# Weight loads ahead of the x loads on two queues, matmuls on zeros before them, and the matmuls for u moved behind the first transposes

## The chip, the cores and the metric

The kernel runs on one core of one Trainium2 chip. The metric is the device time of one execution in microseconds (us); lower is better. Six runs of the kernel before gave a median of 2239.54 us, from 2237.07 to 2243.34.

Names used throughout: PE is TensorE (matmuls and transposes; PEld is its weight load), DVE is VectorE, ACT is ScalarE, POOL is GpSimd, SP is SyncE. SP and ACT each issue DMAs through a hardware queue of their own, POOL through a software queue. Each engine works through its instructions in the order in which they stand in the program.

## The reference

Two layers over 3327 nodes with 512 features. `adj` is a dense 3327 x 3327 matrix.

```python
# layer 0: attention, with adj added twice to the scores
h = maximum(layernorm(x), 0)
q, k, v = h @ Wq.T + bq, h @ Wk.T + bk, h @ Wv.T + bv
a = q @ k.T / sqrt(512) + adj + adj
x = x + softmax(a) @ v
# layer 1: graph convolution
h = maximum(layernorm(x), 0)
A2 = adj + eye
temp = A2 @ h @ W.T
x = x + relu((d[:, None] * A2 * d[None, :]) @ temp)   # d = diagonal(A2) ** -0.5
```

The kernel folds q and k together: the scores need h (Wq.T Wk) h.T, so it forms the 512 x 512 product M = Wq.T Wk once (scaled), and a vector u = Wk.T bq (scaled) that carries the bias. bk adds the same number to a whole row of scores, so softmax drops it.

## The kernel before, in words

All of it is float32. Rows are padded to 26 tiles of 128. The large products (projection of h by M, scores, the three products with adj) are done blockwise in seven products of sums and differences of half matrices in place of eight. That is why one operand always has a step beside the matmuls in which DVE forms sums or differences.

The stages, in order:

1. **Start.** ACT's queue issues the loads of the first six tiles of x (`first`, line 276, 256 KB each). SP's queue issues `bq` (line 154), then the four 128-row pieces of Wq and of Wk in turn (line 285, 256 KB each), then a seventh tile of x, two blocks of adj (line 403, 384 KB each), and then the other 19 tiles of x.
2. **M and u.** PE forms M in 16 matmuls of 512 columns (line 292), with the weight piece `c` as the outer loop and four PSUM banks side by side, so that bank r is complete only in the last of four rounds. The trace shows two passes for each of these matmuls. ACT copies the banks to M in eight pieces (line 296). PE then does 16 one-column matmuls for u (line 300), DVE scales u (line 302), DVE forms four differences of blocks of M (`four_differences`, lines 177 to 180) and ACT negates M[0] in place (line 305). That negation must wait until line 177 has read M[0].
3. **h transposed, and projection.** `h_transposed(k)` (line 307) runs over the tiles of a pack (four packs, 26 tiles). Per tile: mean and variance on DVE (lines 191 to 195), the power on POOL (line 197), the bias `nb` on DVE (line 201), the normalized tile `ht` on ACT (line 314), its store from POOL (line 315), four PE transposes into one of two PSUM banks (line 318), and the copies and sums into `hp` on ACT and DVE (lines 321 to 327). `project_q(k)` (line 329) multiplies a pack by M in chains of products X, Y, Z (line 338), with results gathered on ACT and DVE (lines 343 and 346).
4. **Scores, attention and convolution.** These fill the rest of the time; the change touches none of their code.

Two rings set when the loads of x start: `x_ring` has seven slots, so the load of tile number n + 7 waits until ACT has read tile n at line 314; `n_ring` has four slots for `ht`, so the fifth `ht` waits until the first has been transposed and stored. (Tiles are counted here in the order of their use, from 0.)

The order on each engine is that of a scheduler in this part of the kernel; from the scores on it is fixed by hand. Two places of that order are used in the prediction's steps; they are the same in both kernels. On DVE, the statistics of tile 10 (line 191) with their small follow-ups (lines 193 and 195) stand ahead of the first difference of M (line 177); on ACT, the negation (line 305) stands ahead of the last two copies of M (line 296), and those ahead of the first copy of a transposed tile (line 321).

```python
    x_ring = ring(*((mid, k) for k in range(10, 15)), (half, 13), (half, 14))
    n_ring = ring(*((mid, k) for k in range(4)))
...
    for _ in four_differences(M):
        pass
    nc.scalar.mul(M[0], M[0], -1.0)
```

## Time and profile before

| What | Value |
|---|---|
| Median of 6 runs | 2239.54 us (2237.07 to 2243.34) |
| The profiled execution's own time | 2239.91 us |
| Its span, first to last instruction | 2237.7 us |
| Mean granted TensorE clock | 0.993 |
| DVE busy | 1623.6 us (73% of the span) |
| ACT busy | 230.8 us (10%) |
| DMA, read and written | 583.68 MB, mean 261 GB/s |

The profiled execution's span leaves 2.2 us of its time outside. Times in the trace count from the first instruction. A line of the timeline gives start, length, engine, source line, operation, output and inputs, size and count, and in brackets the idle time of the engine before it with what ended it. A group of instructions in a row is merged into one line; matmuls overlap, so a merged line's length is a little more than the distance to the next start. The view of waits gives, for a pair of waiting and releasing instruction, total time, number of times and the longest.

### The profile page before, as it was taken

The numbers are of one execution on the slowest core, as the hardware profiler recorded it, in microseconds if no ns is written. First come the engines' busy times: TensorE is split into PE (matmuls) and PEld (weight loads), VectorE is DVE, ScalarE is ACT, GpSimd is POOL, SyncE is SP. The second block draws the span as 40 slices with busy tenths as digits, with TensorE's granted clock in tenths as the row PEclk, the third lists the DMA queues.
The fourth block names the chain that finished last, engine by engine and source line by source line (L and its number), as shares of the span: only waits on it lengthen the run. The fifth ranks groups of instructions, "written<-read, shape, count | busy, mean of one in ns | idle before, by whom it ended". The sixth has DMA issues, their size and how long they took to land. (4 is left out here: it accounts for less than half of the span.)

```text
span 2237.7 us, 20973 instructions
## 1 busy us (share of the span) xinstructions
PE 2182.1 (98%) x6252; PEld 1162.8 (52%) x6252; DVE 1623.6 (73%) x3095; ACT 230.8 (10%) x336; POOL 357.0 (16%) x555
## 2 busy tenths in 40 slices
PE   8999999999999999999999999999999999999996
PEld 4555555455555555555444555555554555555553
DVE  6369888788878788877777778886543458776675
ACT  4321121112110000000000000000000000000011
POOL 4223333333321000001222110000000000000001
PEclk9999999999999999999999999999999999999998
DMA  6568888888969898888787899776646458765694
GB/s 246 205 216 301 297 293 285 303 284 303 349 210 331 325 371 287 286 290 279 244 302 240 301 342 354 276 277 205 207 123 205 146 165 304 231 209 175 210 307 147
DMA packets 246412, 583.68 MB, mean 261 GB/s; under 512 B 34770, under 2 KB 105904, under 8 KB 246288
## 3 DMA queue, kind: packets, MB, share of 16 engines
q1 hardware_dynamic: 191968, 399.15, 53.4%
q0 software_dynamic: 45104, 167.88, 19.8%
q10 hardware_dynamic: 9216, 15.21, 2.2%
q8 instruction: 52, 0.85, 0.2%
q14 instruction: 72, 0.59, 0.1%
HBM read 414.28 MB, written 167.85 MB: 260 GB/s over the span
## 5 line engine op out<-in xcount | busy, mean ns | idle before, releaser
L762 PE MATMUL p<-part,b 128*128 128x448 f32 (+1 forms) x3528 | 1255.9, 514 | 7.4 <-DVE part L172 6.2
L762 PEld LDWEIGHTS p<-part,b 128*128 128x128 f32 x3528 | 668.0, 190 | 575.6 <-issue 299.3
L171 DVE TENSOR_TENSOR part<-part 128x896 f32<-128x896 f32 (+1 forms) x252 | 256.6, 1018 | 84.5 <-PE p L762 46.7
L439 PE MATMUL Y<-qt,hp 128*128 128x448 f32 (+1 forms) x832 | 309.1, 514 | 4.4 <-DVE g L443 3.3
L439 PEld LDWEIGHTS Y<-qt,hp 128*128 128x128 f32 x832 | 157.1, 190 | 140.5 <-issue 72.3
L439 PE MATMUL Z<-qt,hp 128*128 128x384 f32 (+1 forms) x416 | 162.6, 513 | 0.0
L173 DVE TENSOR_TENSOR part<-part,part 128x448 f32<-128x448 f32 (+1 forms) x219 | 129.5, 591 | 17.4 <-PE p L762 0.9
L172 DVE TENSOR_TENSOR part<-part,part 128x448 f32<-128x448 f32 (+1 forms) x219 | 129.4, 591 | 7.3
L838 PE MATMUL p<-w,ct 128*128 128x512 f32 x272 | 125.5, 601 | 5.8 <-DVE part L850 4.1
L754 PE MATMUL p<-part,b 128*128 128x448 f32 (+1 forms) x336 | 124.2, 513 | 0.0
L439 PEld LDWEIGHTS Z<-qt,hp 128*128 128x128 f32 x416 | 78.8, 190 | 67.4 <-issue 36.2
L443 DVE SCALAR_TENSOR_TENSOR g<-g,Y 128x384 f32<-128x384 f32 (+1 forms) x156 | 91.4, 586 | 27.3 <-PE Y L439 26.2
L832 POOL DMA_DIRECT2D sum<-job x52 | 28.4, 547 | 486.0 <-DVE job L829 267.8
L797 DVE TENSOR_TENSOR part<-p,part 128x384 f32<-128x384 f32 (+1 forms) x33 | 19.3, 585 | 106.7 <-ACT part L796 57.4
L754 PEld LDWEIGHTS p<-part,b 128*128 128x128 f32 x336 | 63.5, 190 | 53.7 <-issue 32.6
L838 PEld LDWEIGHTS p<-w,ct 128*128 128x128 f32 x272 | 51.9, 192 | 67.7 <-issue 52.0
L796 ACT COPY part<-p 128x384 f32<-128x384 f32 (+1 forms) x33 | 16.5, 499 | 667.4 <-PE p L762 667.4
L439 PE MATMUL X<-qt,hp 128*128 128x384 f32 (+1 forms) x208 | 81.1, 512 | 0.0
L446 ACT ACTIVATE g<-g 128x768 f32<-128x768 f32 (+1 forms) x48 | 43.0, 896 | 353.9 <-DVE g L443 305.7
L838 PE MATMUL p<-w,part 128*128 128x512 f32 x144 | 68.1, 610 | 5.3 <-DVE ct L806 5.3
L431 POOL DMA_DIRECT2D sum<-o x52 | 36.8, 709 | 221.0 <-DVE o L425 155.4
L89 POOL DMA_DIRECT2D out_dram<-r x34 | 18.4, 542 | 306.8 <-DVE r L887 277.5
(157 smaller groups left out, 1867.5 us busy)
## 6 DMA issues: line engine op xcount, KB each, us to landing
part<-sum SPq DMA_DIRECT2D x104, 448.0 KB, 5.1
part<-p SPq DMA_DIRECT2D x91, 448.0 KB, 6.1
part<-sum SPq DMA_DIRECT2D x104, 384.0 KB, 3.5
part<-p SPq DMA_DIRECT2D x91, 384.0 KB, 4.2
part<-in_adjT_dram SPq DMA_DIRECT2D x78, 448.0 KB, 4.7
b<-row SPq DMA_DIRECT2D x234, 128.0 KB, 4.8
part<-in_adjT_dram SPq DMA_DIRECT2D x78, 384.0 KB, 3.7
g<-in_adjT_dram SPq DMA_DIRECT2D x52, 448.0 KB, 4.5
```

The costliest lines, as they stand in the source:

```text
L171: nc.vector.tensor_add(o[:, 0:2], g[:, 0:4:3], g[:, 1:2].to_broadcast([P, 2, g.shape[-1]]))
L172: nc.vector.tensor_add(o[:, 2], o[:, 1], g[:, 0])
L173: nc.vector.tensor_add(o[:, 3], o[:, 2], g[:, 2])
L431: nc.gpsimd.dma_start(self.to(sumd)[:, 0:2], self.o)
L439: nc.tensor.matmul(ps[:, :wd], h_of(self.t, name, k), qt[B[name]][:, k], start=start and k == 0, stop=k == 1, skip_group_check=True)
L443: nc.vector.scalar_tensor_tensor(a[n], a[n], 2.0, ps[:, :wd], op0=ALU.mult, op1=ALU.add if sign > 0 else ALU.subtract)
L446: nc.scalar.activation(g[1], g[1], AF.Exp, **({"bias": pad} if self.t == HALF - 1 else {}))
L754: nc.tensor.matmul(ps[("p2", "p3", "p4", "p8")[k]][:, :w], b[:, z], a[:, 0, y], start=k == 3, stop=True)
L762: nc.tensor.matmul(ps[r][:, :w], b[:, i], m, start=self.t == 0, stop=self.t == PAIRS - 1 and r in ("p1", "p5", "p6", "p7"))
L797: nc.vector.tensor_sub(c22, p["p6"], c11)
L832: nc.gpsimd.dma_start(sumd[self.s][self.j][:, 2 + self.k], self.a)
L838: nc.tensor.matmul(ps, cts[s][y][d][:, k * P : (k + 1) * P], w[d], start=d == 0, stop=d == DC - 1)
```

## The change

It has four parts. (a) The load of `bq` moves from the front of SP's queue behind the weights and x. (b) Wq is loaded from SP's queue and Wk from ACT's, first of all, and the first six tiles of x are put in pairs, one on each queue, behind the second, third and fourth pair of weight pieces. (c) DVE clears a 128 x 128 tile, and PE does eight matmuls of 128 columns on it into PSUM bank 5, which nothing reads. (d) The 16 matmuls for u and their scaling move behind the code of the first pack's `h_transposed`.

```diff
-    nc.sync.dma_start(bq_sb, bq)
...
-    first = {i: load_x(i, nc.scalar) for _, i in order[:6]}
...
+    first = {}
     for c in range(DC):
-        for w, src in ((w_q, wq), (w_k, wk)):
-            nc.sync.dma_start(w[c // 2][:, c % 2], src[c * P : (c + 1) * P])
+        for w, src, queue in ((w_q, wq, nc.sync), (w_k, wk, nc.scalar)):
+            queue.dma_start(w[c // 2][:, c % 2], src[c * P : (c + 1) * P])
+        if c > 0:
+            for (_, i), queue in zip(order[2 * c - 2 : 2 * c], (nc.sync, nc.scalar)):
+                first[i] = load_x(i, queue)
+    nc.sync.dma_start(bq_sb, bq)
...
+    zero = half(12, [P, P], "zero")
+    nc.vector.memset(zero, 0.0)
+    idle = bank(5, "idle")
+    for _ in range(8):
+        nc.tensor.matmul(idle[:, :P], zero, zero, start=True, stop=True)
     ps = [bank(k, "mm") for k in range(DC)]
...
-    pu = bank(4, "pu")
-    for r in range(DC):
-        for c in range(DC):
-            nc.tensor.matmul(pu[:, r : r + 1], w_k[c // 2][:, c % 2, r * P : (r + 1) * P], bq_sb[:, c : c + 1],
-                             start=c == 0, stop=c == DC - 1)
-    nc.vector.tensor_scalar(u, pu[:, :DC], scale, None, op0=ALU.mult)
...
     h_transposed(TURN[0])
+    pu = bank(4, "pu")
+    for r in range(DC):
+        for c in range(DC):
+            nc.tensor.matmul(pu[:, r : r + 1], w_k[c // 2][:, c % 2, r * P : (r + 1) * P], bq_sb[:, c : c + 1],
+                             start=c == 0, stop=c == DC - 1)
+    nc.vector.tensor_scalar(u, pu[:, :DC], scale, None, op0=ALU.mult)
```

In the order of the built programs, part (d) puts the matmuls for u behind the transposes of tiles 0 and 1, and the scaling of u behind the sums of tile 1 (lines 324 and 325). From the projection on, every engine has the same instructions in the same order in both kernels.

## The prediction

> **What bounds the kernel now.** I read the page first, then busy time by stretches, then PE's waits at the start, then the timeline of the first 40 us.

> ```profile
> span 2237.7 us, 20973 instructions
> ...
> PE 2182.1 (98%) x6252; PEld 1162.8 (52%) x6252; DVE 1623.6 (73%) x3095; ACT 230.8 (10%) x336; POOL 357.0 (16%) x555
> ```

> PE is busy for 98% of the span, so only PE's idle or slow time can be won. Busy time by stretches (length, then PE, PEld, DVE and so on) says how much of it lies where the change acts:

> ```profile
> 0.00:66.62 66.62, 54.31 (x221) 32.78 (x221) 41.89 (x147) 35.88 (x65) 30.63 (x60) 1.00 0.71 254
> 66.62:2237.70 2171.08, 2127.78 (x6033) 1130.06 (x6031) 1581.74 (x2950) 194.96 (x271) 326.36 (x496) 0.99 0.76 261
> ```

> Up to 66.62 us PE idles 12.31 us. After that it runs instructions that the change leaves in place, so whatever is won must be won here and then shifts all the rest. PE's waits in the first 75 us name those 12 us:

> ```profile
> PE mm L292 <- DMA wk<-in_wk_dram: 6.9, 1, 6.9
> PE tp L318 <- DVE hp L325: 2.3, 2, 1.9
> PE Z L338 <- DVE hp L324: 1.6, 1, 1.6
> PE tp L318 <- ACT hp L321: 1.0, 2, 0.8
> ```

> The first is what the change aims at. The timeline shows what follows it:

> ```profile
> 6.94 16.06 PE L292 MATMUL mm<-wk,wq 128*128 128x512 f32 x32 [6.94 <-DMA wk<-in_wk_dram]
> ...
> 10.48 0.34 PEld L292 LDWEIGHTS mm<-wk,wq 128*128 128x128 f32 x1 [0.52 <-issue]
> ...
> 11.25 0.19 PEld L292 LDWEIGHTS mm<-wk,wq 128*128 128x128 f32 x1 [0.43 <-issue]
> ...
> 20.55 0.69 DVE L191 BATCH_NORM_STATS2 st<-xt 128x6 f32<-128x512 f32 x1
> ...
> 22.01 0.69 DVE L177 TENSOR_TENSOR M<-M 128x512 f32<-128x512 f32 x1 [0.36 <-ACT M L296]
> ...
> 22.73 0.63 ACT L305 ACTIVATE M<-M 128x512 f32<-128x512 f32 x1
> 22.83 3.63 PE L300 MATMUL pu<-bq_sb,wk 128*128 128x1 f32 x32
> ...
> 26.32 1.07 PE L318 MATMUL tp<-ident,ht 128*128 128x128 f32 x8
> ...
> 26.99 0.58 ACT L321 COPY hp<-tp 128x512 f32<-128x512 f32 x1 [3.08 <-PE tp L318]
> ...
> 27.63 0.66 PE L318 MATMUL tp<-ident,ht 128*128 128x128 f32 x4 [0.24 <-ACT hp L321]
> ```

> Three things: the passes at line 292 start 0.85 us apart at first and 0.43 apart from 11.25 on, so PE ran at half rate for the first 4.2 us or so of its work; 32 passes took 15.89 us instead of 32 x 0.43 = 13.76. Second, the copy at 26.99 waited for PE, that is for u. Third, DVE reads tile 10 at 20.55, as it lands, and goes on to line 177 only then. That third thing hides behind u now; I think it decides the result.

> **The change part by part.**

> *Weights first.* The first weights land 3.7 us (Wq) and 5.2 us (Wk) after their issue, the second one at 6.8. They share the transfer with six tiles of x; landings come about 0.67 to 0.7 us apart (14 of 256 KB by 12.9). As the first pair on two queues from 0.74 on, they land where the first two transfers landed before: the first x at 3.7, the second landing at 4.9. [...] Later pairs, every 1.4 us or 2.8 with x between, are ahead of the 3.44 us that eight passes take.

> *Zero matmuls.* DVE's other memsets end at 0.99; the new one adds an estimated 0.15, before any x has landed. Eight matmuls are 16 passes of 128 columns. At the slow rate that is 0.855/4 = 0.21 each, by twice the 0.11 of the transposes 0.22: 3.5 us from about 1.3, to 4.85. So M starts at 4.9, not 6.94. If they ran at full rate, the landing sets it, 3.8 to 4.9; if each were twice as dear, 8.4, a loss of 1.5. The transposes' row is nearest, so 4.9. The clock: 4.2 us after 1.3 is 5.5, so (5.5 - 4.9)/2 = 0.3 us of loss remain of the 2.1. [...] I take 0.3. M ends at 4.9 + 13.76 + 0.3 = 19.0 instead of 22.83: 3.85 us won there.

> *u behind the transposes.* No work is saved: 32 passes, 3.49 us, only change places. The eight transposes come at 19.0 to 19.9, u to 23.4; then tile 2, which stood at 27.63. If nothing else held it, the gain would be 4.2. `bq` is needed at 19.9 and its landing, some 8 us earlier, is hidden. On DVE, u's scaling now stands behind tile 1's sums; behind it are two `nb`, which wait for POOL later anyway: nothing.

> *x behind weights: the price.* Tile 2's transposes need the bank that the copy at line 321 frees. On ACT that stands behind the negation (305), that behind DVE's line 177, that behind the statistics of tile 10. So when does tile 10 land? Before, `nb` for the first four tiles came after the sixth x (10.94); in the new DVE order it follows the fifth, on SP the seventh transfer, so about the fourteenth of all: 12.87 before, say 12.3 without the slow first us. `ht` of tile 0 then starts at 13.1 (11.81 before), that of tile 3 ends at 16.0 (14.74), and tile 10's load, which waits for it, is issued at 16.0:

> ```profile
> L272 SPq DMA_DIRECT2D xt<-in_x_dram x1: 328/328/328, 14.8 to 14.8; - x1
> ...
> DMA to landing us min/median/max: 5.8/5.8/5.8
> ```

> ```profile
> 10.00:20.00 10.00, 10.00 (x23) 4.31 (x22) 4.92 (x24) 2.93 (x4) 5.08 (x9) 1.00 1.04 391
> 20.00:30.00 10.00, 8.96 (x59) 6.76 (x58) 4.87 (x15) 6.02 (x15) 1.12 (x2) 1.00 0.02 6
> ```

> Those 5.8 us are a full queue (DMA share 1.04, then 0.02), not a latency. The amount in front of tile 10 is the same, so its landing moves less than its issue: bound 19.5 (queue never empty, 0.3 us won at the front and more overlap) to 21.8 (16.0 + 5.8). A small gap opens while x waits for `ht`; I take 20.3. POOL's powers for tiles 4 to 7, which wait for the later stores, let DVE arrive at about the same time. Then 1.1 us to line 177 (20.55 to 21.64 without its wait), 0.7 to the negation, 0.55 to the last copies of M, 0.6 of them: 23.25 for the copy at 321 instead of 26.99. Tile 2's transposes go at 23.25 + 0.6 = 23.9 instead of 27.63: **3.75 us**, 0.45 less than PE alone would give. From there ACT, DVE, POOL and the next loads follow tile 2 as before: the 0.80 us wait, the 1.61 at Z and the 2.3 later come back unchanged, with about 1 us of doubt in Z, where two loads took 5.0 and 4.4 us.

> *Sum:* 2239.91 - 3.75 = 2236.2 for the profiled execution, which is 0.37 above the median; against the median 2235.8. A measurement of this kernel tells about 0.2% (4.5 us) from no change, so the forecast lies just inside: the bound is 2235.06.

> **The rivals.**

> A, the sum above: gain 2.7 to 4.8, 2234.7 to 2236.8, chance 0.52. About 0.18 of that is a gain over 4.5, by a shorter wait at Z.

> B, tile 10 doesn't gate. It lands by 19.7, or DVE's wait disappears in part; PE's 4.2 us hold, and with loads less crowded a good part of the 1.61 us at Z goes: 5.0 to 6.5, about 2234. For it: the DMA engines stand idle from 21 to 28 us, so loads could be quicker. Against: they are full before. Chance 0.24.

> [...] With other half losses, chance 0.14.

> D, slower. Tile 10 lands so late that the copy at 321 comes after 26.99; each us from a landing of 24.0 on costs one us. That needs 8.0 us from its issue at 16.0, where the longest of the 256 KB loads took 6.0; or the fifth x at 14.5 and 6.0 on top of that. Landing at 27: 3 us lost, 2242.5. For it: three more loads in front of the fifth x. Chance 0.10, of which 0.06 over 0.2%.

> **How the numbers follow.** The likeliest is A: 2235.8. The range takes in B and C: 2233.0 to 2239.0, leaving D and the tail of B. Faster by over 0.2%: B and the good end of A, 0.42; slower 0.06; within 0.2%, 0.52.

> **What would show it.** First pass at line 292 near 4.9 us with PEld 0.19 long at once (step of the zeros); PE's first wait in the list gone; the next start after M's last pass near 19.0. Tile 10's statistics near 20.3 with DVE idle ahead of them, line 305 near 22, and a wait of about half a us of tile 2's transposes for the copy at 321. If that wait isn't there and tile 2 goes at 23.4, B. [...] If the copy comes after 27, D. I'd also be wrong if something after 66.62 us reacts to the shift.

## The result, and the profile after

The changed kernel takes 2235.68 us, the median of 32 runs (2229.05 to 2239.77). The kernel before, run beside it, takes 2239.83 us, the median of 69 runs. The ratio is 0.998, with a 95% interval of 0.9974 to 0.9986, which is a gain of 3.1 to 5.8 us. The forecast was 2235.8 us, 3.75 us less than before.

Line numbers move a little: in the changed kernel the matmuls for M are line 302 (292 before), M's copies 306 (296), the negation 309 (305), `ht` 318 (314), the transposes 322 (318), the copy out of their bank 325 (321), the sums behind it 328 and 329 (324 and 325), Z 342 (338). The zero matmuls are line 298, those for u line 368. DVE's first difference of M is line 176 and its statistics line 190.

The head of the page, after:

```profile
span 2232.6 us, 21006 instructions
...
PE 2184.5 (98%) x6268; PEld 1167.5 (52%) x6268; DVE 1622.6 (73%) x3096; ACT 230.9 (10%) x336; POOL 357.9 (16%) x555
```

PE is busy 2.4 us longer in a span that is 5.1 us shorter: the 16 zero passes are new work. Busy time by stretches, after (length, then PE, PEld, DVE, ACT, POOL, and at the end clock, DMA share and GB/s):

```profile
0.00:66.62 66.62, 60.78 (x244) 39.20 (x245) 43.80 (x150) 36.01 (x65) 31.42 (x61) 0.95 0.76 264
```

PE's idle time in the first 66.62 us falls from 12.31 to 5.84 us. These 6.47 us are not the gain: from 1.15 to 4.72 us PE now does zeros, 3.57 us that count as busy. And the mean clock is down from 1.00 to 0.95. The clock's first record stands at 11.14 us before and at 5.34 after, and this column counts what lies ahead of it as full: it doesn't show the slow start at all, and the drop to 0.95 is the first sign of something else, which the forecast lacked. PE's waits of the first 75 us, after:

```profile
PE tp L322 <- DVE hp L329: 2.1, 2, 1.7
PE Z L342 <- DVE hp L328: 1.4, 1, 1.4
PE idle L298 <- DVE mh L621: 1.1, 1, 1.1
PE tp L322 <- ACT hp L325: 1.1, 2, 0.7
```

The 6.9 us for `wk` are gone; in their place stands the 1.1 us until DVE's memsets are done, and everything below has hardly changed. PE's timeline, after:

```profile
1.15 3.78 PE L298 MATMUL idle<-zero 128*128 128x128 f32 x16 [1.15 <-DVE mh L621]
4.72 14.21 PE L302 MATMUL mm<-wk,wq 128*128 128x512 f32 x32
18.77 1.04 PE L322 MATMUL tp<-ident,ht 128*128 128x128 f32 x8
19.64 4.30 PE L368 MATMUL pu<-bq_sb,wk 128*128 128x1 f32 x32
24.34 1.11 PE L322 MATMUL tp<-ident,ht 128*128 128x128 f32 x4 [0.40 <-ACT hp L325]
```

M runs from 4.72 to 18.77 us. The passes for u take 4.30 us where they took 3.63. Tile 2's transposes, the last line, wait 0.40 us for ACT and start at 24.34 instead of 27.63 us: 3.29 us won there. What ACT and DVE do ahead of that is seen in their timelines, after:

```profile
20.91 0.69 DVE L190 BATCH_NORM_STATS2 st<-xt 128x6 f32<-128x512 f32 x1
...
21.93 0.68 DVE L176 TENSOR_TENSOR M<-M 128x512 f32<-128x512 f32 x1
```

```profile
22.64 0.63 ACT L309 ACTIVATE M<-M 128x512 f32<-128x512 f32 x1 [3.87 <-DVE M L176]
23.17 0.64 ACT L306 ACTIVATE M<-mm 128x256 f32<-128x256 f32 x2
23.70 0.59 ACT L325 COPY hp<-tp 128x512 f32<-128x512 f32 x1
24.17 0.40 ACT L327 COPY hp<-tp 128x256 f32<-128x256 f32 x1
24.43 0.84 ACT L318 ACTIVATE ht<-xt,nb,rstd 128x512 f32<-128x512 f32 x1
```

Tile 10 of x lands at 20.89, DVE takes it at once, and ACT stands still for 3.87 us until the first difference of M is done. Then ACT works without a gap. PE had filled the first bank by about 19.4 us; the copy out of it came at 23.70. So the chain from tile 10 to tile 2 is there as forecast. Busy time by short stretches, after, shows the lost clock:

```profile
20.00:22.00 2.00, 2.00 (x20) 2.00 (x20) 1.89 (x9) 0.00 (x0) 0.00 (x0) 1.00 0.40 151
22.00:23.00 1.00, 1.00 (x9) 1.00 (x8) 0.60 (x2) 0.36 (x1) 0.00 (x0) 0.71 0.00 0
23.00:29.00 6.00, 4.92 (x19) 3.91 (x20) 3.49 (x10) 5.29 (x12) 2.42 (x5) 0.50 0.39 103
29.00:30.00 1.00, 1.00 (x4) 0.44 (x4) 0.72 (x3) 1.00 (x2) 0.98 (x2) 0.88 0.87 336
```

The granted clock is at half from 22.41 to 29.24 us, 6.83 us long, beginning while PE works on u without a break. In the first profile of before it was full from 11.14 us on, up to 1065.86 us. The 3.29 us won at tile 2 shrink to 2.50 at the first Y (27.93 against 30.43). At the first Z they are 2.18 (34.73 against 36.91), but there PE waits for a load of x. DVE's timeline, after:

```profile
33.66 0.69 DVE L190 BATCH_NORM_STATS2 st<-xt 128x6 f32<-128x512 f32 x1 [1.58 <-DMA xt<-in_x_dram]
34.27 0.40 DVE L328 TENSOR_TENSOR hp<-hp,tp 128x256 f32<-128x256 f32 x1
```

These are the statistics of tile 13, which landed at 33.63, and the sums that Z needs stand behind them on DVE. In six profiles (this one, after_again, gate10, no_u_move, loads_only and zeros_only) the first Z starts 1.09 to 1.10 us behind the landing of tile 13. So 0.8 us, from tile 2 to Y, is what the half clock took here; what follows is set by a load. From 66 to 560 us the gain stays at 2.41 us.

The two profiled spans differ by 5.1 us, though, not 2.4. The rest comes later, in steps of up to 1.7 us in both directions. One cause is half-clock stretches of different length (near 2013 us, 6.83 us before and 3.41 after); not every step has one. Two executions of the changed kernel differ in the same way: the distance of after and after_again moves between -1.5 and +0.9 us behind 200 us. A single pair of profiles therefore shows where time went in the first 66 us; what the change is worth is read from the medians.

### The profile page after: what moved, and what is told of

Read it like the earlier page. It is cut to its first block, busy times and chain, and to the rows that moved or that the text cites. A ratio compares the mean times of both kernels' runs of the same rounds, so it can differ in the third digit from the quotient of the medians.

```text
span 2232.6 us, 21006 instructions
## 1 busy us (share of the span) xinstructions
PE 2184.5 (98%) x6268; PEld 1167.5 (52%) x6268; DVE 1622.6 (73%) x3096; ACT 230.9 (10%) x336; POOL 357.9 (16%) x555
```

## The experiments

The theory at the outset: (1) the early weights and the zeros win 3.85 us at M; (2) moving u wins nothing, because (3) tile 10's landing, through DVE's order and the negation, sets tile 2; (4) the half clock behind u takes about 1.2 us back. The rivals: the gain comes from the early loads or the zeros alone; moving u is needed; tile 10's gate costs little; the half clock has nothing to do with u.

A table of what all profiles show, in us from the first instruction. "Gate" is the landing of the tile of x whose statistics stand last ahead of the first difference of M (tile 10, but tile 9 in gate10, none in gate8 and its kin). "Copy" is the first copy out of the transposes' bank.

| Kernel | ratio to before (95% interval) | M starts | last of u | gate | negation | copy | tile 2 | half clock from, for |
|---|---|---|---|---|---|---|---|---|
| before | | 6.94 | 26.21 | 20.53 | 22.73 | 26.99 | 27.63 | none |
| before_again | | 7.41 | 26.46 | 21.24 | 22.99 | 27.25 | 27.89 | 28.24, 6.83 |
| after | 0.998 (0.9974 to 0.9986) | 4.72 | 23.59 | 20.89 | 22.64 | 23.70 | 24.34 | 22.41, 6.83 |
| after_again | one run | 4.72 | 23.57 | 21.31 | 23.06 | 24.12 | 24.76 | 21.96, 10.24 |
| loads_only | 0.9992 (0.9983 to 1.0001) | 4.56 | 25.18 | 21.31 | 23.36 | 26.53 | 27.17 | 23.17, 10.24 |
| zeros_only | 0.9988 (0.9979 to 0.9997) | 6.38 | 23.57 | 20.10 | 22.13 | 24.35 | 24.99 | 25.07, 6.83 |
| u_only | 0.9998 (0.9989 to 1.0007) | 6.61 | 26.09 | 20.45 | 22.20 | 23.27 | 26.20 | 26.54, 6.83 |
| no_u_move | 0.9981 (0.9972 to 0.9989) | 4.52 | 21.90 | 22.52 | 24.42 | 25.48 | 26.12 | 21.37, 10.24 |
| gate10 | 0.9973 (0.9965 to 0.9982) | 4.72 | 23.57 | 21.53 | 23.29 | 24.35 | 24.99 | 21.98, 10.24 |
| gate8 | 0.996 (0.9948 to 0.9972) | 4.72 | 23.59 | none | 19.98 | 21.05 | 23.80 | 22.35, 6.83 |
| gate8_again | 0.9957 (0.9944 to 0.997) | 4.72 | 23.60 | none | 20.08 | 21.15 | 23.81 | 22.54, 6.83 |
| gate8_wide32 | 0.9959 (0.9943 to 0.9975) | 4.43 | 25.16 | none | 20.86 | 21.93 | 22.57 | 24.59, 6.83 |
| no_move_wide | 0.9993 (0.9984 to 1.0002) | 4.72 | 22.19 | 21.15 | 23.19 | 24.25 | 24.89 | 29.15, 3.41 |

### The parts alone

**loads_only**: before with the new order of loads, parts (a) and (b). From the changed kernel:

```diff
-    zero = half(12, [P, P], "zero")
-    nc.vector.memset(zero, 0.0)
-    idle = bank(5, "idle")
-    for _ in range(8):
-        nc.tensor.matmul(idle[:, :P], zero, zero, start=True, stop=True)
...
+    pu = bank(4, "pu")
...
     for _ in four_differences(M):
...
     h_transposed(TURN[0])
-    pu = bank(4, "pu")
```

> Only parts (a) and (b): weights first on two queues, x between them, bq last; no zero matmuls, u in its old place. My theory: M starts when the first pair lands (4.3 us), at the half rate for its first 4 us or so (2.1 us lost), ends near 20.2; u to 23.7; the first copy of a transposed tile after that; tile 2's transposes near 25.0 instead of 27.63, so 2.7 us won there, total 2237.1. Rival (x behind weights delays all that follows): tile 2 at 27 or later, no gain. Rival (the loads bring everything): tile 2 near 24.3, as in the whole change, total 2236.

Measured: 2237.92 us, ratio 0.9992 (0.9983 to 1.0001). M started at 4.56 us and ended at 20.84, 0.3 and 0.6 us later than expected; full clock came only 4.96 us after its first pass. Tile 2 was forecast for 25.0 and came at 27.17: the half clock began at 23.17, so u took 4.56 us up to the first transpose (3.49 in the first profile of before), and the transposes came 0.22 us apart (0.11 in after, from 18.77 to 19.64). The early loads alone win 2 us at M. At the end the gain is between -0.2 and 3.8 us, which can't be told from nothing.

**zeros_only**: before with part (c).

```diff
+    zero = half(12, [P, P], "zero")
+    nc.vector.memset(zero, 0.0)
+    idle = bank(5, "idle")
+    for _ in range(8):
+        nc.tensor.matmul(idle[:, :P], zero, zero, start=True, stop=True)
     ps = [bank(k, "mm") for k in range(DC)]
```

> Only part (c): zero matmuls ahead of M, loads and u as before. My theory: M still waits for its weights until 6.9 us but runs at full rate from there, ends near 20.7 instead of 22.8; tile 2's transposes near 25.5: 2.2 us won there, total 2237.6. Rival (zeros do not wake the clock, or it falls asleep again in the 2 us before the weights land): M ends at 22.8, 0 won.

Measured: 2237.25 us, ratio 0.9988 (0.9979 to 0.9997), and tile 2 at 24.99 where 25.5 was expected. M started at 6.38 and its last pass at 19.76 us: 13.38 us for 31 distances, that is 0.43 each from the first on. The zeros do warm the clock, and that alone is a gain, of 0.7 to 4.7 us. (That M started 0.56 us earlier than in the first profile of before is an earlier landing in this execution; the loads are the same.)

**u_only**: before with part (d).

```diff
-    pu = bank(4, "pu")
...
     h_transposed(TURN[0])
+    pu = bank(4, "pu")
...
```

> Only part (d): u's matmuls behind the first transposes, loads as before, no zeros. My theory: PE's order costs nothing and wins nothing by itself but the wait of 0.24 us ahead of tile 2; tile 2's transposes near 27.2 instead of 27.63, total 2239.3, within the noise of before. Rival (the copies of the first tiles, done beside u now, take over the 0.8 us wait behind it too): 1.0 to 1.2 us won at the first product Y.

Measured: 2238.66 us, ratio 0.9998 (0.9989 to 1.0007). Copies at 23.27 wait for nothing that PE does any more, and tile 2 comes right behind u, at 26.20. A pass earlier or later there is nothing: u's 3.5 us only change places with the transposes. That the profile shows 1.4 us at tile 2, a us more than expected, comes with an M that ended 1 us earlier in this execution (last pass at 21.41 against 22.41): its weights landed 0.3 us earlier, and full clock came 2.86 us after its first pass instead of 4.20.

**no_u_move**: all but part (d). From the changed kernel:

```diff
+    pu = bank(4, "pu")
...
     for _ in four_differences(M):
...
     h_transposed(TURN[0])
-    pu = bank(4, "pu")
```

> The whole change without part (d): loads and zeros new, u in its old place ahead of the transposes. My theory (the first copy of a transposed tile is held by DVE's statistics of tile 10, not by PE): PE has u done by 22.3 and transposes tiles 0 and 1 by 23.2, in the shadow of that copy at 23.7; tile 2's transposes at 24.3, the same as in the whole change, total equal to it within 0.5 us (2235.7). Rival (moving u wins its share): tile 2 about 0.9 us later, at 25.2.

Measured: 2235.72 us, ratio 0.9981 (0.9972 to 0.9989), the same as the whole change. So moving u can't be told from nothing, both alone and on top of the rest; each time the interval is some 2 us wide to either side. Tile 2 came 1.8 us later in this profile than expected. PE was done with u and the first transposes by 24.1, well before the copy at 25.48; tile 10 had landed late, at 22.52, and DVE had waited for the tile before it:

```profile
21.89 0.69 DVE L190 BATCH_NORM_STATS2 st<-xt 128x6 f32<-128x512 f32 x1 [2.14 <-DMA xt<-in_x_dram]
...
23.70 0.68 DVE L176 TENSOR_TENSOR M<-M 128x512 f32<-128x512 f32 x1
```

The negation followed at 24.42, the copy at 25.48 (1.06 later) and tile 2 at 26.12 (0.64 later): the chain of the forecast with other numbers at its head.

Loads and zeros together are worth 0.0019, by these medians about what they are worth one by one (0.0008 + 0.0012, each with 0.0009 to either side).

### Is it tile 10 that gates?

**gate10**: the changed kernel with one ordering more on DVE: the statistics of tile 10 stand behind the sums of tile 1. Only these statistics and their small follow-ups change their place; up to 87 us nothing else does on any engine, as the traces show.

```diff
+    def newest():
+        return nc.cur_bb.bb.instructions[-1]
+
+    gates, seen = [], []
     def norm(src):
         nc.vector.bn_stats(st, src)
+        seen.append(src)
+        if len(seen) == LATE and gates:
+            tc.add_manual_dep(newest(), gates[0],
+                              mybir.DependencyInfo(mybir.DependencyClass.NoSync, mybir.DependencyReason.DATA),
+                              reason="behind the sums of tile 1")
...
                 nc.vector.tensor_add(hp[k][:, 5, :, w], hp[k][:, 0, :, w], pt[:, 0:2])
+                gates.append(newest().name)
```

Here `LATE` is 11, so tile 10 alone is moved.

> The whole change, with one difference in DVE's order: the statistics of tile 10 stand behind tile 1's sums and no longer ahead of the first difference of M; nothing is left out. My theory (DVE's wait for x holds the negation, that the copies of M, those the first copy of a transposed tile): the gate is tile 9 now, which lands about 1 us earlier. The negation follows tile 9's landing by 1.8 to 2.0 us as it followed tile 10's before; at a landing of 19.9 it is at 21.7, tile 2's transposes near 23.4 instead of 24.3. Total 0.5 to 1 below the whole change, about 2235. Rival (PE's own order holds tile 2): no change at tile 2.

Measured: 2234.34 us, ratio 0.9973 (0.9965 to 0.9982); its interval overlaps that of the change, so no gain is shown. Tile 2 was expected at 23.4 and came at 24.99, later than in the changed kernel: the loads of x were late in this execution, and tile 9 landed at 21.53, not at 19.9. But the gate passed on to tile 9 as expected: the negation came 1.76 us after its landing, where it had come 1.75 us after tile 10, and only 1.22 us after that of tile 10 (22.07), which no longer stands in its way. A different tile with the same distance speaks for the mechanism; gate8 tests it by taking the gate away.

**gate8**: the same with `LATE` at 9 and the condition `LATE <= len(seen) <= 11`, so that tiles 8, 9 and 10 stand behind the sums of tile 1. Tiles 0 to 7 have their statistics done before M is.

> As the last, with the statistics of tiles 8, 9 and 10 behind tile 1's sums; nothing is left out. My theory: nothing of DVE waits for x ahead of the differences; the negation comes at 18.5 to 19 (when ACT has M[0] and M[1] ready and tile 7's bias is done, by 19.5 at the latest), the first copy by 20.6, and now PE is what holds tile 2: its transposes follow u's last pass at 23.2 (23.7 if the clock falls to half in u). Total 1 to 1.5 below the whole change, about 2234.5. Rival (PE's order, or the statistics coming later cost as much): tile 2 at 24.3, or the first product Z later than in the whole change.

Measured: 2230.94 us, ratio 0.996 (0.9948 to 0.9972): 3.6 us below what was expected, better than both kernels, and its interval lies just apart from that of the change. ACT's timeline, gate8 (line 320 is the negation, 336 the copy, 329 `ht`):

```profile
19.98 0.63 ACT L320 ACTIVATE M<-M 128x512 f32<-128x512 f32 x1 [1.25 <-DVE M L177]
...
21.05 0.59 ACT L336 COPY hp<-tp 128x512 f32<-128x512 f32 x1
...
21.78 0.84 ACT L329 ACTIVATE ht<-xt,nb,rstd 128x512 f32<-128x512 f32 x1
```

The wait ahead of the negation falls from 3.87 to 1.25 us, though tile 10 landed at 20.89 us again: the negation, at 19.98, is now ahead of it. It still came 0.5 us later than the latest time expected. PE now sets tile 2: u's last pass starts at 23.59, tile 2's first at 23.80. That is only 0.54 us earlier than in the changed kernel, and yet the first Z starts at 32.99, 1.74 us earlier. The lead is 0.95 us at 55 us and 2.75 us from 66 us on. PE's waits of the first 75 us, gate8:

```profile
PE idle L309 <- DVE mh L633: 1.1, 1, 1.1
PE tp L333 <- DVE hp L340: 1.0, 1, 1.0
PE tp L333 <- ACT hp L336: 0.9, 2, 0.7
```

The 1.4 us at Z are gone. Gone too are the 1.7 us for line 329's sum, which PE waited at 61 us in the changed kernel; in return gate8 waits 1.0 us for such a sum at 52 us. One cause is in ACT's queue: `ht` of tile 4 stands behind the negation and the copies, at 24.43 us in the changed kernel and at 21.78 in gate8, and it frees the slot of `x_ring` for tile 11. That load is issued at 25.30 against 22.65 us, and the loads behind it are less crowded: tile 13, for which Z waited, lands at 31.49 instead of 33.63 us, though it is issued only 0.56 us earlier. The view of line 271 of the changed kernel, from 21 to 30 us, has who waited for these loads and the time from issue to landing:

```profile
  DVE st L190: 2.2, 2
...
DMA to landing us min/median/max: 2.7/4.4/5.0
```

In gate8 nobody waits for them, and the landing takes 3.1 us at the median. But there is a second cause, which this run can't separate from the first. The scheduler placed more than the three statistics differently, on all four engines behind 24 us: in gate8 tile 13's statistics stand at 36.11 us, behind the sums for Z (31.76), and no longer ahead of them. So a late negation costs 0.5 to 1 us at tile 2 (against after and after_again). That it costs again at Z by way of the ring is likely, and how much of the 1.4 us is not shown.

**gate8_again**: the same kernel once more.

> gate8 as before, beside the wider u on one chip and as a repetition: 2230.9 (ratio to the kernel before 0.996), negation not tied to the landings of tiles 9 and 10, tile 2's transposes 0.2 us behind u's last pass, near 23.8. If the first result owed something to its chip, the ratio comes out nearer to that of the whole change, 0.998.

Measured: 2231.47 us, ratio 0.9957 (0.9944 to 0.997), negation at 20.08, tile 2 at 23.81. It repeats, on another chip.

### Does u cost the clock?

**before_again**: the kernel before, once more, for its profile.

> The kernel before, unchanged, for a second profile. Theory of the clock: the half clock after u belongs to all versions and the first profile of before, which showed none, was the exception; here a stretch of 6.8 or 10.2 us at half clock begins between 23 and 30 us. Then the first product Y, at 30.4 in the first profile, is 1 to 2 us later. Rival (before never has it, the change brings it): full clock up to 1000 us, Y at 30.4 again.

Measured: 2241.62 us, one run. The stretch from 28 to 35 us, in this second profile of before:

```profile
28.00:35.00 7.00, 6.32 (x21) 4.39 (x22) 3.99 (x14) 5.02 (x10) 4.51 (x8) 0.52 0.65 213
```

The clock is 0.52 here, and 1.00 in the same stretch of the first profile. So the half clock behind u is no work of the change: four of the five profiles with u in its old place have it (this one, loads_only, zeros_only and no_u_move), and the first profile of before is the exception. It cost less here than expected: the first Y came at 31.18, 0.75 us later than in the first profile. Against this second profile the changed kernel is 2.4 + 2.7 = 5.1 us ahead at 100 us, against the first 2.4 us; the medians' 4.15 us lie between. Most of these 2.7 us are not the clock behind u: the two profiles of before differ by 0.7 us at 55 us, and the rest comes by 80 us, with longer waits of PE for DVE's sums (2.2 us in place of 1.9) and another half-clock stretch at 65.79 us.

**after_again**: the changed kernel, once more.

> The changed kernel once more, for a second profile of it. If the half clock behind u is a property of the kernel (one-column passes that leave TensorE nearly idle for the clock gate), a stretch of 6.8 or 10.2 us at half clock starts again between 21.4 and 25 us. If the first profile caught a chance event, there is none before 60 us. Tile 10 of x gates in both: negation = landing of tile 10 + 1.75 to 2.05 us, first copy = negation + 1.06, tile 2's transposes 0.6 later; by the landings seen so far (20.9 to 22.5) they start between 24.3 and 26.2. Its time: 2235.7, one run, so 2231 to 2240 says nothing.

Measured: 2233.99 us, one run. Half clock from 21.96 us for 10.24 us, negation 1.75 us behind tile 10, copy 1.06 later, tile 2 at 24.76: all as expected. Ten of the eleven profiles with u in one-column passes have the stretch.

**no_move_wide**: all but part (d), and u's matmuls 128 columns wide. The moving operand is the column of bq repeated 128 times, and one column of each result is used.

```diff
-            nc.tensor.matmul(pu[:, r : r + 1], w_k[c // 2][:, c % 2, r * P : (r + 1) * P], bq_sb[:, c : c + 1],
-                             start=c == 0, stop=c == DC - 1)
-    nc.vector.tensor_scalar(u, pu[:, :DC], scale, None, op0=ALU.mult)
+            nc.tensor.matmul(pu[:, r * P : (r + 1) * P], w_k[c // 2][:, c % 2, r * P : (r + 1) * P],
+                             bq_sb[:, c : c + 1].to_broadcast([P, P]), start=c == 0, stop=c == DC - 1)
+    nc.vector.tensor_scalar(u, pu[:, 0 : BW : P], scale, None, op0=ALU.mult)
```

> The whole change without part (d), and u's matmuls 128 columns wide (the same column read 128 times), of which one is used; nothing is left out. Theory of the clock: a stretch of PE with only one-column passes counts as idle, so that the clock falls to half after u (it did in five of six profiles: from 21.4 for 10.2 us in the kernel with one-column passes). With wide passes, which should take the same 0.11 us each, u counts as work: the clock stays full through u and 3.4 us more, so no half clock before 25.8, or none at all; total 1 to 2 below that kernel's 2235.7. Rival (the fall is a matter of chance or of other causes): half clock from 21 to 25 again, same total.

Measured: 2238.62 us, ratio 0.9993 (0.9984 to 1.0002). That is 4 to 5 us above what was expected, and above its kin no_u_move (0.9981), though the intervals overlap. The profiled execution, 2230.36 us, is the fastest of the 14. The passes started at 18.73 to 22.19 us, 0.11 us apart like the narrow ones. The stretch behind u, no_move_wide:

```profile
22.00:29.00 7.00, 3.14 (x26) 2.46 (x24) 4.67 (x17) 4.92 (x11) 2.31 (x4) 1.00 0.27 85
```

The clock stays full, though PE is busy for only 3.14 of these 7 us, where the changed kernel was busy for 4.92 of 6 us and had half. That speaks for the width of the passes as what counts, not for PE's busy time; a count in the last section bears it out. The 3.4 us that the expectation adds behind u are the author's estimate; 3.41 us is what the shortest half-clock stretch of after lasts, and here the half clock came 6.96 us behind the start of u's last pass. But it is one profile, a half-clock stretch comes later in it (29.15 us, behind these waits of PE), and its time can't be used: with the other operand the scheduler put the transposes, ACT's and DVE's steps around u in another order, and PE waited 1.56 us for the copy and 1.62 us for DVE's sums behind it. It doesn't show what the half clock behind u costs.

**gate8_wide32**: gate8, with u 32 columns wide; only PE's order changes, tile 2's transposes going between u's passes.

```diff
-            nc.tensor.matmul(pu[:, r : r + 1], w_k[c // 2][:, c % 2, r * P : (r + 1) * P], bq_sb[:, c : c + 1],
+            nc.tensor.matmul(pu[:, r * P : r * P + 32], w_k[c // 2][:, c % 2, r * P : (r + 1) * P],
+                             bq_sb[:, c : c + 1].to_broadcast([P, 32]), start=c == 0, stop=c == DC - 1)
-    nc.vector.tensor_scalar(u, pu[:, :DC], scale, None, op0=ALU.mult)
+    nc.vector.tensor_scalar(u, pu[:, 0 : BW : P], scale, None, op0=ALU.mult)
```

> gate8 with the matmuls for u 32 columns wide instead of one (the moving operand is bq's column repeated 32 times; only one column of each result is used). If it is the width of the moving operand that the clock gate counts, more work per pass shortens or removes the half clock behind u: full clock through 22 to 30 us, up to 1.5 us less than gate8, 2229.5. If 32 columns are still too few, the half clock stays as in gate8 (6.8 us from about 22.4) and the time is the same, 2230.9. A rival: the half clock has nothing to do with u; then also the same. u's passes stay at 0.11 us each in all cases; if they are longer, the time is up to 1 us more, 2232.

Measured: 2230.1 us, ratio 0.9959 (0.9943 to 0.9975), not to be told from gate8. The half clock is still there, from 24.59 for 6.83 us. PE waited 1.80 us for a copy between u's passes here, so the profile alone does not say whether 32 columns are too few or that wait brought the half clock; by the estimate in the last section 32 are too few either way.

## Why the prediction was right, point by point

**Weights first.** Forecast: landing between 3.8 and 4.9; the first two loads of this size landed at 3.77 and 4.92 before. They landed at 4.11 (Wq, SP's queue) and 4.27 (Wk, ACT's queue), nearer to the lower of these bounds. No run has both weights on one queue, so what the second queue is worth was not shown. Without zeros (loads_only) M began at 4.56.

**Zeros.** Forecast: 16 passes from 1.3 to 4.85 us at 0.21 each, M from 4.9, 0.3 us of half clock left, M's end at 19.0. Measured: 1.15 to 4.72, 0.22 each, full clock from 5.34, which is (5.34 - 4.72)/2 = 0.31 us, M's end at 18.77. The step was right; that it fits so closely is luck. The forecast took the 4.2 us from first work to full clock in one profile for a fixed length. In the thirteen profiles it is anything from 2.86 us (u_only) to 4.96 us (loads_only), so it is no fixed length. In the eight profiles with new loads and zeros the loss that remains at M is 0 to 0.4 us; none of them shows the greater losses to which the forecast gave a chance of 0.14.

**u moved.** Forecast: nothing but an exchange of places. By the medians it is nothing that 2 us of interval would show: 0.998 with it, 0.9981 without, 0.9998 alone.

**Tile 10 as the price.** Forecast: landing at 20.3 (bounds 19.5 to 21.8), line 177 1.1 us later, the negation 0.7 later, the copy at 23.25, tile 2 at 23.9 with a wait of about half a us: 3.75 us won. Measured: 20.89, then 1.02, 0.71 and 1.06 us, copy at 23.70, tile 2 at 24.34 with a wait of 0.40 us: 3.29 us won. Every link held. The term that was off is the landing: the load was issued at 15.91 (forecast 16.0) and took 5.0 us, not 4.3. In the second profile it was 21.31, so such landings spread by some tenths from one execution to the next, and the result with them.

**The later waits come back unchanged.** They did: 0.80, 1.61 and 1.9 us became 0.7, 1.4 and 1.7. The forecast put the wait at Z down to two slow loads, and a load it is: tile 13's. But it took these loads for independent of the gate. Gate8 shows a link, by way of `ht` of tile 4 and the ring, without showing how much of the wait hangs on it. So the forecast's price of the gate, 0.45 us, was too low for what can be won there: with the gate gone (and the order behind it changed) the medians improve by about 0.002, some 4.5 us, of which the profiles show 2.7 us (after) to 4.2 us (after_again) by 200 us of the run. Rival B put a kernel without the gate at about 2234; gate8 came to 2230.9.

**What the forecast lacked** is the half clock behind u, 0.8 us between tile 2 and the first Y. It doesn't spoil the number, because the profiles with u in its old place have it too, four of five; the sum was made against the one in which it was missing. Against that profile 2.4 us remain; the medians, which average over such differences, give 4.15 us. That the forecast's 3.75 lies so near the median is therefore partly luck: a landing 0.6 us late, and a reference profile with a better clock than the others, work in opposite directions.

**The bound of 0.2%.** The forecast put the change just inside it; the measured ratio is 0.998, and its interval has the bound in its middle. By the medians loads and zeros each give part, though the loads alone are not told from nothing, and only together do they reach it.

## What to carry to other kernels

When PE's first wait is shortened, follow ACT and DVE to the instruction that stands in front of the next release of a PSUM bank: here a statistic of x that nobody needed yet stood ahead of it in DVE's order, and moving three such steps back (gate8) gained about as much again as the whole change, though the scheduler moved other steps with them. A wait that returns unchanged after a shift is not thereby independent; look whether it hangs, through a ring of buffers, on the step that held the first one up. Profile the kernel before twice when the gain looked for is about 0.1% (2.2 us here): two executions of it differed by 2.7 us within the first 100 us.

## What the runs showed of the hardware that was not expected

```profile
2.12 0.43 SPq L285 DMA_DIRECT2D wq<-in_wq_dram  x1
...
4.12 0.33 SPq L271 DMA_DIRECT2D xt<-in_x_dram  x1
```

In before, ACT's fifth issue came at 3.43 us, ahead of the landing of ACT's first load (3.77) and right behind that of `bq` on SP's queue (3.41), whose semaphore it takes over.
